# Third stage of a four-stage layer: whole score blocks below the diagonal in four 32-row tiles, numerators split in every fourth step

## The chip, the cores and the metric

The kernel runs on one core of a Trainium2 chip. The metric is the time of one execution on the device in microseconds (us). Five engines run their own instruction queues in order: PE multiplies matrices (PEld is its loading of the stationary operand), DVE, ACT and POOL work on vectors, SP issues transfers.

## The reference

The input is a tensor of 2 batches x 1024 tokens x 128 features, held in fp32. Four blocks follow one another, each as x = x + LN(block(LN(x))), with LN a layer norm without gain. The change touches the third block alone, a causal attention with 16 heads of 8 features and a linear position bias:

```
q = (x @ Wq + bq).reshape(B, S, 16, 8)          # k and v alike
scores = einsum('bthd,bshd->bhts', q, k) / sqrt(8)
scores = scores - slope[h] * |s - t|            # slope 2**(-8/16*(h+1))
scores = where(s > t, -inf, scores)
out = einsum('bhts,bshd->bthd', softmax(scores), v).reshape(B, S, 128)
return out @ Wo + bo
```

The first block is a non-causal attention with 8 heads, the second a mixture of experts, the fourth two layers of a local attention with a gated feed-forward part.

## The kernel before

The stages `phase1` to `phase4` run one after another. `phase3` (from line 705) works on eight groups u = 0 to 7: two batches times four groups of four heads. Lines named here are those of the kernel before.

**Operands.** `make(u, "q")` and `make(u, "k")` (lines 821 to 844) project the tokens of one batch onto the four heads of a group. They use three matmuls for each half of 512 tokens (high and low parts of both operands, `mm3`). The weights hold every head's 8 columns three times, so that the stacked operand `stk` (128 rows x 1024 tokens, fp16) has 32 rows of rounded values, 32 rows that are either the rounding's rest or a second copy, 32 more of this kind, and in rows 96 to 127 constants loaded from memory (`c_rows3`). These are 8 rows a head: the position bias in pieces, and one row that carries minus the row maximum. One product over 128 rows thus gives four heads' scores added up. To keep the heads apart, k is copied four times into `kz`, each copy multiplied by a column of `pick` that is zero outside one head's rows (lines 838 to 842, two of the four on POOL and two on DVE, except in the first group, where DVE does all).

**Maxima.** `max_pass` (lines 853 to 869) computes scores with the queries on the partitions, 128 queries by up to 512 keys. Blocks on the diagonal get the causal mask by a second matmul (line 864). DVE reduces each bank to a negative maximum (line 869). `units` lists the pieces of a group, 38 in all. `max_rows(u, c)` (lines 871 to 879) transposes the maxima of one half of the queries on PE into partitions 96 to 127 of a bank, and one ACT copy writes them from there into rows 96 to 127 of q.

**Scores.** `scores(n)` (lines 883 to 904) computes one step: 12 steps a group, step (c, j) for query half c and key block j of 128, with the keys on the partitions. Steps (0, 0) to (0, 3) and (1, 4) to (1, 7) touch the diagonal; (1, 0) to (1, 3) are whole blocks of 512 queries. There are four matmuls, one for each head, against `kz`; ACT's exponential (line 898) reads the bank into `pt`, of which there are four buffers. In every second step ACT copies `pt` to fp16 (line 902) and POOL subtracts (line 903): `hl` holds a high and a low part.

**Values.** `values(n)` (lines 906 to 931) multiplies by V, four heads side by side in 32-column tiles: with `hl`, two fp16 passes against V in fp16; without, `pt` and V in fp32. A `pt` without `hl` is free again only after this. `outputs` (line 933) divides by the sums and, after its matmuls (line 942), writes the result.

**Order.** The main loop (lines 977 to 1003) runs over steps m from -12 to the end. The maxima run 12 steps ahead of the scores and the values four steps behind them:

```
            if 0 <= m < steps:
                put(scores, m)
            ...
            for unit in rows:
                put(max_rows, *unit)
            ...
            if 0 <= m - 4 < steps:
                put(values, m - 4)
            while done < len(todo) and done < (u + 1) * len(units) / 12:
                put(max_pass, *todo[done])
```

Here `u` is m + 12, and after the maxima come `make` for the next group (at steps 3 and 5 of twelve), `finish` and `outputs`. `put` chains PE's instructions, so PE follows the written order. The order on ACT, DVE, POOL and SP is set by a planner from planned times, within the dependences. `k.tick` (line 1003) lets the fourth stage's preparation in from m = 54 on: loads on SP (line 1056 is its weights'), and on POOL and ACT the splitting of weights (lines 1058 to 1063).

**Banks.** `bank()` (line 786) takes PSUM banks in turn from two pools of three. In the last 14 steps it takes them from one pool of three only.

Of the kernel before, what the change touches and what calls it, by code (L numbers as in the profile page):

```python
# [704 lines left out]
def phase3(k, X):  # L705
# [5 lines left out]
    with ExitStack() as es:  # L711
# [14 lines left out]
        bias = cp.tile([96, 2, G], F32, name="bias")  # L726
        nc.sync.dma_start(bias, A["t_bqk3"])
        scale = HD**-0.5
        nc.vector.tensor_scalar(bias[:, 0, :], bias[:, 0, :], scale, None, ALU.mult)
        bvo = cp.tile([128, 2, D], F32, name="bvo")  # L730
        for i, n in enumerate(("bv", "bo")):
            nc.sync.dma_start(bvo[:, i, :], A["L1_attn_" + n].partition_broadcast(128))
        wqk = {}
        for i, n in enumerate("qk"):
            w = work().rearrange("p t d -> p (t d)")[:, : G * 96].rearrange("p (g m) -> p g m", g=G)
# [85 lines left out]
        def make(u, n):  # L821
            b, g = u // G, u % G
            xTh, xTl = S["x", b]
            wh, wl = wqk[n]
            i = 0 if n == "q" else 1
            stk = qp.tile([128, N], F16, name=n + "st", bufs=3 if n == "q" else 1)
            S["dma"] = nc.sync.dma_start(stk[96:128, :], A["c_rows3"][i, g])
            bc = bias[:, i, g : g + 1]
            lo = slice(32, 64) if n == "q" else slice(64, 96)
            for c in range(2):  # L830
                s = slice(512 * c, 512 * c + 512)
                ps = bank()
                k.mm3(ps[:96, :], wh[:, g, :], wl[:, g, :], xTh[:, s], xTl[:, s])
                nc.scalar.activation(stk[:96, s], ps[:96, :], AF.Identity, bias=bc)
                nc.vector.scalar_tensor_tensor(stk[lo, s], ps[lo, :], bc[lo, :], stk[lo, s], ALU.add, ALU.subtract)
            if n == "k":
                kz = qp.tile([128, 4, N], F16, name="kz")
                for a in range(4):
                    if u and a < 2:
                        S["kz"] = nc.gpsimd.tensor_scalar(kz[:, a, :], stk, pick[:, a : a + 1], None, ALU.mult)  # L840
                    else:
                        nc.vector.tensor_scalar(kz[:, a, :], stk, pick[:, a : a + 1], None, ALU.mult)
                stk = kz
            S[n, u] = stk


        units = []
        for t in range(NT):
            for e in range(t // 4 + 1):
                m = {1: 4, 2: 2}.get(t + 1 - 4 * e, 1)  # L850
                units += [(t, e, a, m) for a in range(0, 4, m)]

        def max_pass(u, i):
            t, e, a0, m = units[i]
            n = 128 * min(4, t + 1 - 4 * e)
            ps = bank().rearrange("p (a n) -> p a n", a=m)
            q0, kz = S["q", u], S["k", u]
            diag = e == t // 4
            for a in range(m):
                nc.tensor.matmul(  # L860
                    ps[:, a, :n], q0[:, 128 * t : 128 * t + 128], kz[:, a0 + a, 512 * e : 512 * e + n], start=True, stop=not diag
                )
                if diag:
                    nc.tensor.matmul(ps[:, a, n - 128 : n], identb, causal[:, 0, :], start=False, stop=True)  # L864
            if e == 0:
                out = mx[:, u % G, t, :].rearrange("p (a r) -> p a r", r=8)[:, a0 : a0 + m, 6]
            else:
                out = mx2[:, u % 2, t - 4, a0 : a0 + m]
            S["max"] = nc.vector.tensor_reduce(out, ps[:, :, :n], AX.X, ALU.max, negate=True)  # L869
# [12 lines left out]

        def scores(n):
            u = n // 12
            c, j = order[n % 12]
            q1, kz = S["q", u], S["k", u]
            s = max(512 * c, 128 * j)
            w = 512 * c + 512 - s
            diag = j >= 4 * c
            pt = pp.tile([128, 4, 512], F32, name="pt")  # L890
            m = {128: 4, 256: 2}.get(w, 1)
            for a0 in range(0, 4, m):
                st = bank().rearrange("p (a n) -> p a n", a=m)
                for a in range(m):
                    nc.tensor.matmul(st[:, a, :w], kz[:, a0 + a, 128 * j : 128 * j + 128], q1[:, s : s + w], start=True, stop=not diag)  # L895
                    if diag:
                        nc.tensor.matmul(st[:, a, :128], identb, causal[:, 1, :], start=False, stop=True)  # L897
                S["exp"] = nc.scalar.activation(pt[:, a0 : a0 + m, :w], st[:, :, :w], AF.Exp)  # L898
            hl = None
            if n % 2 == 0:  # L900
                hl = pp.tile([128, 2, 4, 512], F16, name="hl", bufs=2)
                nc.scalar.copy(hl[:, 0, :, :w], pt[:, :, :w])  # L902
                nc.gpsimd.tensor_tensor(hl[:, 1, :, :w], pt[:, :, :w], hl[:, 0, :, :w], ALU.subtract)  # L903
            S["p", n] = pt, hl, s, w
# [65 lines left out]
        ahead = 12  # L970
        for n in "qk":
            make(0, n)
        done = 0
# [585 lines left out]
def consts():  # L1559
# [26 lines left out]
    c["c_pick3"] = (np.arange(128)[:, None] // 8 % 4 == np.arange(4)).astype(np.float32)  # L1586
# [46 lines left out]
def layouts(inputs):  # L1633
# [11 lines left out]
    w = np.stack([a["L1_attn_" + n].reshape(128, 4, 1, 32) for n in ("Wq", "Wk")], 1)  # L1645
    c["t_wqk3"] = np.repeat(w, 3, 3).reshape(128, 2, 4, 96)
    w = np.stack([a["L1_attn_" + n].reshape(4, 32) for n in ("bq", "bk")])
    c["t_bqk3"] = np.concatenate([w, w, w], 2).transpose(2, 0, 1)
# [29 lines left out]
```

## Time and profile before

| | |
|---|---|
| time, median of 3 runs | 1354.97 us (1350.28 to 1356.17) |
| profiled execution | 1356.68 us |
| its span (first to last instruction) | 1354.9 us |
| mean granted TensorE clock | 0.945 |
| busy, share of the span | PE 86%, PEld 53%, DVE 72%, ACT 71%, POOL 62% |
| chain that ended last, by engine | PE 42%, DVE 29%, ACT 14%, issue 6%, POOL 4%, DMA 3% |
| line 898, exponentials | x304, 480 to 668 ns |
| line 869, maxima | x304, 540 to 700 ns |
| line 902, copies of the numerators | x48, 1045 to 1980 ns |
| line 903, their rests on POOL | x48, 2125 to 4095 ns |
| line 827, constant rows | x16, 64 KB each, 1.8 us from issue to landing |

All durations come from the one profiled execution. A matmul's duration holds its way through the array; matmuls that follow each other closely start sooner than that, so distances between starts are given where they matter. Line 49, 50 and 51 are the helper `mm3`, which all stages use. The windows give, for a stretch of the span, how long each engine was busy.

### The profile page before, as it was taken

The page shows a single profiled execution, that of the slowest core. Times are in us where ns is not written, and L with a number is a line of the kernel's source. Part 1 is how long each engine was busy: PE and PEld are TensorE (multiplying, and loading weights), DVE is VectorE, ACT ScalarE, POOL GpSimd, SP SyncE. Part 2 cuts the span into 40 slices and gives each one's busy share as a digit, 9 for nine tenths or more (in the row PEclk, how much of TensorE's full clock was granted, in tenths as well). Part 3 has the DMA queues.
Part 4 walks back from the last instruction along what each step waited for, and adds up shares of the span by engine and source line. Part 5 has one row for each costly group of instructions (what it writes and reads, how often), then busy time and mean ns, then how long its engine had stood idle before and what let it go on. Part 6 is the DMA issues. An engine that isn't in the chain of part 4 may idle for free.

```text
span 1354.9 us, 28455 instructions
## 1 busy us (share of the span) xinstructions
PE 1162.4 (86%) x11558; PEld 716.5 (53%) x11558; DVE 982.3 (72%) x1970; ACT 958.2 (71%) x1481; POOL 842.6 (62%) x525
## 2 busy tenths in 40 slices
PE   4799999999897889887799998798668898998886
PEld 1366666666565646443355544343336565666564
DVE  6777666776674385989888789571578887888855
ACT  2777777787686364541898987789367788887755
POOL 1666667777665463733676768785577886666611
PEclk8899999999898999998999999898679899999999
DMA  2000000000000031300000013000157666555520
GB/s 77 1 2 2 2 2 1 2 17 18 1 1 2 18 131 32 112 13 4 3 5 3 5 38 73 1 21 1 24 94 163 122 119 106 103 99 100 106 59 16
DMA packets 123394, 57.59 MB, mean 43 GB/s; under 512 B 105568, under 2 KB 114800, under 8 KB 123264
## 3 DMA queue, kind: packets, MB, share of 16 engines
q1 hardware_dynamic: 121360, 54.50, 18.7%
q8 instruction: 90, 1.47, 0.4%
q10 hardware_dynamic: 1472, 1.09, 0.3%
q0 software_dynamic: 432, 0.20, 0.2%
q14 instruction: 40, 0.33, 0.1%
HBM read 21.69 MB, written 1.11 MB: 17 GB/s over the span
## 4 chain that ended last, share of the span: by engine, by line
PE 42%; DVE 29%; ACT 14%; issue 6%; POOL 4%; DMA 3%; SPq 0%; POOLq 0%; DVEq 0%; ACTq 0%
DVE mx L869 5%; PE big L360 5%; PE pu L49 4%; PE pu L51 3%; PE pu L50 3%; DVE nm L332 3%; PE pu L920 3%; ACT pt L898 2%; PE big L49 2%; PE big L51 2%; PE big L50 2%; PE bank L895 1%; PE bank L860 1%; PE big L656 1%; DVE ln_st L81 1%
## 5 line engine op out<-in xcount | busy, mean ns | idle before, releaser
L367 POOL TENSOR_TENSOR hl<-p,hl 128x1024 f16<-128x1024 f32 x128 | 274.0, 2143 | 142.8 <-ACT hl L366 116.2
L903 POOL TENSOR_TENSOR hl<-pt,hl 128x2048 f16<-128x2048 f32 (+1 forms) x48 | 164.4, 3432 | 78.1 <-ACT hl L902 68.4
L332 DVE TENSOR_REDUCE nm<-big 128x2 f32<-128x1024 f32 x128 | 155.2, 1220 | 32.3 <-PE big L329 31.6
L364 ACT ACTIVATE p<-big 128x1024 f32<-128x1024 f32 x128 | 130.9, 1023 | 52.4 <-PE big L360 51.6
L49 PEld LDWEIGHTS <-hl 128*128 128x128 f16 x1024 | 100.5, 98 | 75.7 <-DVE acc L392 43.6
L366 ACT CAST hl<-p 128x1024 f16<-128x1024 f32 x128 | 133.8, 1045 | 4.1
L869 DVE TENSOR_REDUCE mx<-bank 128x1 f16<-128x512 f32 (+3 forms) x157 | 102.1, 653 | 32.1 <-PE bank L860 16.4
L869 DVE TENSOR_REDUCE mx<-bankz 128x1 f16<-128x512 f32 (+3 forms) x147 | 96.6, 660 | 18.7 <-PE bankz L864 12.8
L898 ACT ACTIVATE pt<-bank 128x512 f32<-128x512 f32 (+1 forms) x172 | 97.0, 582 | 18.5 <-PE bank L897 11.1
L49 PE MATMUL pu<-V1h,hl 128*128 128x129 f16 x512 | 92.6, 224 | 12.4 <-DVE acc L392 11.7
L49 PE MATMUL pu<-V0h,hl 128*128 128x129 f16 x512 | 93.1, 224 | 10.8 <-DVE acc L392 9.5
L50 PEld LDWEIGHTS <-hl 128*128 128x128 f16 x1024 | 101.3, 99 | 0.0
L1221 POOL TENSOR_TENSOR rot<-rot,rn 128x512 f32<-128x512 f32 x64 | 66.3, 1056 | 55.8 <-DVE rn L1211 50.4
L51 PEld LDWEIGHTS <-hl 128*128 128x128 f16 x1024 | 100.5, 98 | 0.0
L1196 POOL TENSOR_TENSOR rot<-rot,t 128x512 f32<-128x512 f32 x64 | 84.1, 1326 | 20.2 <-DVE t L1190 20.1
L51 PE MATMUL pu<-V0h,hl 128*128 128x129 f16 x512 | 92.5, 223 | 0.0
L50 PE MATMUL pu<-V0l,hl 128*128 128x129 f16 x512 | 92.5, 222 | 0.0
L51 PE MATMUL pu<-V1h,hl 128*128 128x129 f16 x512 | 92.0, 222 | 0.0
L50 PE MATMUL pu<-V1l,hl 128*128 128x129 f16 x512 | 92.0, 221 | 0.0
L898 ACT ACTIVATE pt<-bankz 128x512 f32<-128x512 f32 (+1 forms) x132 | 76.8, 583 | 20.8 <-PE bankz L897 9.9
L88 POOL TENSOR_TENSOR ln_rstd<-ln_rs,nhalf 128x4 f32<-128x4 f32 (+2 forms) x29 | 32.8, 1135 | 81.4 <-DVE ln_rs L84 67.3
L895 PE MATMUL bank<-qst,kz 128*128 128x512 f16 (+3 forms) x218 | 68.1, 345 | 13.5 <-DVE mx L869 7.5
(412 smaller groups left out, 3730.9 us busy)
## 6 DMA issues: line engine op xcount, KB each, us to landing
sb<-sd SPq DMA_DIRECT2D x16, 512.0 KB, 4.4
Vs<-V SPq DMA_DIRECT2D x60, 130.0 KB, 2.4
work<-in_t_w SPq DMA_DIRECT2D x2, 512.0 KB, 3.5
out<-F SPq DMA_DIRECT2D x3, 256.0 KB, 2.3
X<-in_L_attn_x SPq DMA_DIRECT2D x2, 256.0 KB, 3.3
w<-in_t_wqk SPq DMA_DIRECT2D x1, 512.0 KB, 5.1
wv<-in_t_wv ACTq DMA_DIRECT2D x1, 512.0 KB
X<-in_L_attn_x ACTq DMA_DIRECT2D x1, 512.0 KB, 5.0
```

The lines of the kernel that those rows point to most:

```text
L49: mm(out, lh, rh, start=start, stop=False, **kw)
L50: mm(out, lh, rl, start=False, stop=False, **kw)
L51: mm(out, ll, rh, start=False, stop=stop, **kw)
L332: S["red"] = nc.vector.tensor_reduce(S["n", u][:, i // 2, c, :], ps, AX.X, ALU.max, negate=True)
L364: S["exp"] = nc.scalar.activation(p, st, AF.Exp, scale=QSCALE**-2)
L366: nc.scalar.copy(hl[:, 0], p)
L367: S["lo"] = nc.gpsimd.tensor_tensor(hl[:, 1], p, hl[:, 0], ALU.subtract)
L869: S["max"] = nc.vector.tensor_reduce(out, ps[:, :, :n], AX.X, ALU.max, negate=True)
L895: nc.tensor.matmul(st[:, a, :w], kz[:, a0 + a, 128 * j : 128 * j + 128], q1[:, s : s + w], start=True, stop=not diag)
L898: S["exp"] = nc.scalar.activation(pt[:, a0 : a0 + m, :w], st[:, :, :w], AF.Exp)
L903: nc.gpsimd.tensor_tensor(hl[:, 1, :, :w], pt[:, :, :w], hl[:, 0, :, :w], ALU.subtract)
L1196: eng("ra" if j else "rb", i).tensor_tensor(rot[:, j], rot[:, j], t2[:, j], ALU.add)
```

## The change

The rows of the operands are put in another order. Each head now has 32 adjacent rows: three times its 8 features (rounded values and rests) and its 8 constant rows. The weights get a fourth, empty set of columns, so that a projection fills all 128 rows. ACT writes the projection, multiplied by a column `low` that is one on the rows that need the rest, into a new tile `hi`; one DVE pass over 128 rows then makes `stk` out of both. The constant rows come after that, by four transfers of 8 rows each. `k`'s operand gets three buffers and is kept beside `kz`.

A new helper `four` takes the four heads of a whole block: four matmuls over 32 rows each, in four tile positions, into four banks, and then the four readers. Whole blocks in `max_pass` and `scores` use it with the unmultiplied operand; blocks on the diagonal keep `kz`. In `units` a whole block is now one unit with a load of 4, and the loop counts loads. `max_rows` copies the maxima to a tile `mr`, from which four transfers on SP take them to q's rows. The numerators are split where n is a multiple of 4.

```diff
+        low = cp.tile([128, 2], F32, name="low")
+        nc.sync.dma_start(low, A["c_low3"])
...
+        lbias = cp.tile([128, 2, G], F32, name="lbias")
+        nc.vector.tensor_tensor(lbias, bias, low.unsqueeze(2).to_broadcast([128, 2, G]), ALU.mult)
...
-            h = cp.tile([128, G, 96], F32R, name=n + "wh")
-            l = cp.tile([128, G, 96], F32R, name=n + "wl")
+            h = cp.tile([128, G, 128], F32R, name=n + "wh")
+            l = cp.tile([128, G, 128], F32R, name=n + "wl")
...
-            stk = qp.tile([128, N], F16, name=n + "st", bufs=3 if n == "q" else 1)
-            S["dma"] = nc.sync.dma_start(stk[96:128, :], A["c_rows3"][i, g])
+            stk = qp.tile([128, N], F16, name=n + "st")
             bc = bias[:, i, g : g + 1]
-            lo = slice(32, 64) if n == "q" else slice(64, 96)
             for c in range(2):
                 s = slice(512 * c, 512 * c + 512)
                 ps = bank()
-                k.mm3(ps[:96, :], wh[:, g, :], wl[:, g, :], xTh[:, s], xTl[:, s])
-                nc.scalar.activation(stk[:96, s], ps[:96, :], AF.Identity, bias=bc)
-                nc.vector.scalar_tensor_tensor(stk[lo, s], ps[lo, :], bc[lo, :], stk[lo, s], ALU.add, ALU.subtract)
+                k.mm3(ps, wh[:, g, :], wl[:, g, :], xTh[:, s], xTl[:, s])
+
+                hi = qp.tile([128, 512], F16, name="hi", bufs=2)
+                nc.scalar.activation(hi, ps, AF.Identity, scale=low[:, i : i + 1], bias=lbias[:, i, g : g + 1])
+                nc.vector.scalar_tensor_tensor(stk[:, s], ps, bc, hi, ALU.add, ALU.subtract)
+            for a in range(4):
+                S["dma"] = nc.sync.dma_start(stk[32 * a + 24 : 32 * a + 32, :], A["c_rows3"][i, g, 8 * a : 8 * a + 8])
...
+        def four(l, r, w, use):
+
+            tiles = [bank() for _ in range(4)]
+            for a, ps in enumerate(tiles):
+                d = slice(32 * a, 32 * a + 32)
+                nc.tensor.matmul(ps[:, :w], l[d, :], r[d, :], start=True, stop=True, tile_position=(32 * a, 0))
+            for a, ps in enumerate(tiles):
+                use(a, ps[:, :w])
...
-                m = {1: 4, 2: 2}.get(t + 1 - 4 * e, 1)
+                m = {1: 4, 2: 2}.get(t + 1 - 4 * e, 1) if e == t // 4 else 4
                 units += [(t, e, a, m) for a in range(0, 4, m)]
+        load = [4 if e < t // 4 else 1 for t, e, *_ in units]
...
+            if e < t // 4:
+                four(q0[:, ts], kst[:, 512 * e : 512 * e + n], n, lambda a, ps: reduce(a, ps.unsqueeze(1)))
+                return
...
-            nc.scalar.copy(S["q", u][96:128, 512 * c : 512 * c + 512], ps[96:128, :])
+            mr = qp.tile([128, 512], F16, name="mr", bufs=2)
+            nc.scalar.copy(mr[96:128, :], ps[96:128, :])
+            q = S["q", u][:, 512 * c : 512 * c + 512]
+            for a in range(4):
+                nc.sync.dma_start(q[32 * a + 24 : 32 * a + 32, :], mr[96 + 8 * a : 104 + 8 * a, :])
...
+            if not diag:
+                four(kst[:, ks], q1[:, s : s + w], w, lambda a, ps: exp(a, ps.unsqueeze(1)))
...
-            if n % 2 == 0:
+            if n % 4 == 0:
                 hl = pp.tile([128, 2, 4, 512], F16, name="hl", bufs=2)
...
-            while done < len(todo) and done < (u + 1) * len(units) / 12:
+            while done < len(todo) and spent < (u + 1) * sum(load) / 12:
                 put(max_pass, *todo[done])
+                spent += load[todo[done][1]]
                 done += 1
```

More of the change, by code (lines that the diff above doesn't have):

```diff
@@ L725, in phase3 @@
         nc.sync.dma_start(both, A["c_both3"])
-        bias = cp.tile([96, 2, G], F32, name="bias")
+        low = cp.tile([128, 2], F32, name="low")
+        nc.sync.dma_start(low, A["c_low3"])
+        bias = cp.tile([128, 2, G], F32, name="bias")
         nc.sync.dma_start(bias, A["t_bqk3"])
@@ L734, in phase3 @@
         for i, n in enumerate("qk"):
-            w = work().rearrange("p t d -> p (t d)")[:, : G * 96].rearrange("p (g m) -> p g m", g=G)
+            w = work().rearrange("p t d -> p (t d)")[:, : G * 128].rearrange("p (g m) -> p g m", g=G)
             nc.sync.dma_start(w, A["t_wqk3"][:, i])
-            h = cp.tile([128, G, 96], F32R, name=n + "wh")
-            l = cp.tile([128, G, 96], F32R, name=n + "wl")
+            h = cp.tile([128, G, 128], F32R, name=n + "wh")
+            l = cp.tile([128, G, 128], F32R, name=n + "wl")
             if n == "q":
@@ L842, in make @@
                         nc.vector.tensor_scalar(kz[:, a, :], stk, pick[:, a : a + 1], None, ALU.mult)
-                stk = kz
+                S["z", u] = kz
             S[n, u] = stk
+        def four(l, r, w, use):
[5 more added lines that the diff above has]
+                use(a, ps[:, :w])
         units = []
@@ L855, in max_pass, with reduce @@
             n = 128 * min(4, t + 1 - 4 * e)
+            q0, kst, kz = S["q", u], S["k", u], S["z", u]
+            if e == 0:
+                out = mx[:, u % G, t, :].rearrange("p (a r) -> p a r", r=8)[:, :, 6]
+            else:
+                out = mx2[:, u % 2, t - 4, :]
+            ts = slice(128 * t, 128 * t + 128)
+            def reduce(a, ps):
+                S["max"] = nc.vector.tensor_reduce(out[:, a : a + ps.shape[1]], ps, AX.X, ALU.max, negate=True)
+            if e < t // 4:
+                four(q0[:, ts], kst[:, 512 * e : 512 * e + n], n, lambda a, ps: reduce(a, ps.unsqueeze(1)))
+                return
             ps = bank().rearrange("p (a n) -> p a n", a=m)
-            q0, kz = S["q", u], S["k", u]
-            diag = e == t // 4
             for a in range(m):
[L860 to L869, printed above, removed]
+                nc.tensor.matmul(ps[:, a, :n], q0[:, ts], kz[:, a0 + a, 512 * e : 512 * e + n], start=True, stop=False)
+                nc.tensor.matmul(ps[:, a, n - 128 : n], identb, causal[:, 0, :], start=False, stop=True)
+            reduce(a0, ps[:, :, :n])
         def max_rows(u, c):
@@ L885, in scores @@
             c, j = order[n % 12]
-            q1, kz = S["q", u], S["k", u]
+            q1, kst, kz = S["q", u], S["k", u], S["z", u]
             s = max(512 * c, 128 * j)
@@ L890, in scores, with exp @@
             pt = pp.tile([128, 4, 512], F32, name="pt")
+            ks = slice(128 * j, 128 * j + 128)
+            def exp(a, ps):
+                S["exp"] = nc.scalar.activation(pt[:, a : a + ps.shape[1], :w], ps, AF.Exp)
+            if not diag:
+                four(kst[:, ks], q1[:, s : s + w], w, lambda a, ps: exp(a, ps.unsqueeze(1)))
             m = {128: 4, 256: 2}.get(w, 1)
-            for a0 in range(0, 4, m):
+            for a0 in range(0, 4 if diag else 0, m):
                 st = bank().rearrange("p (a n) -> p a n", a=m)
                 for a in range(m):
[L895 to L898, printed above, removed]
+                    nc.tensor.matmul(st[:, a, :w], kz[:, a0 + a, ks], q1[:, s : s + w], start=True, stop=False)
+                    nc.tensor.matmul(st[:, a, :128], identb, causal[:, 1, :], start=False, stop=True)
+                exp(a0, st[:, :, :w])
             hl = None
-            if n % 2 == 0:
+            if n % 4 == 0:
                 hl = pp.tile([128, 2, 4, 512], F16, name="hl", bufs=2)
@@ L972, in phase3 @@
             make(0, n)
-        done = 0
+        done = spent = 0
         later = chain(tokens(1), values_of(1))
@@ L1585, in consts @@
     c["c_mx3"] = mx.reshape(128, 4, NT, 32)
-    c["c_pick3"] = (np.arange(128)[:, None] // 8 % 4 == np.arange(4)).astype(np.float32)
+    c["c_pick3"] = (np.arange(128)[:, None] // 32 == np.arange(4)).astype(np.float32)
+    part = np.arange(128) % 32 // 8
+    c["c_low3"] = np.stack([part == 1, part == 2], 1).astype(np.float32)
     both = np.zeros((128, 4, 9), np.float32)
@@ L1644, in layouts @@
     c["t_wv"] = a["L0_attn_Wv"].reshape(8, 128, 128).transpose(2, 0, 1)
[L1645 to L1648, printed above, removed]
+    three = lambda v: np.concatenate([v, v, v, np.zeros_like(v)], -1)
+    w = np.stack([a["L1_attn_" + n].reshape(128, 4, 4, 8) for n in ("Wq", "Wk")], 1)
+    c["t_wqk3"] = three(w).reshape(128, 2, 4, 128)
+    w = np.stack([a["L1_attn_" + n].reshape(4, 4, 8) for n in ("bq", "bk")])
+    c["t_bqk3"] = three(w).reshape(2, 4, 128).transpose(2, 0, 1)
     pad = lambda v: np.concatenate([v, np.zeros((*v.shape[:-1], 384 - v.shape[-1]), v.dtype)], -1)
```

## The prediction

> **What bounds the kernel now.** The page gives no single answer (PE 86%, DVE 72%, ACT 71%, POOL 62% of the span), so I read the third stage by windows. Its matmuls begin at 601 us and end at 964 us. Scores start at 641, and seven of the eight head groups run with the maxima of the next group beside them until 917; the eighth runs alone.
>
> ```profile
> 655.00:674.20 19.20, 17.12 (x123) 7.63 (x122) 15.71 (x26) 17.53 (x29) 12.93 (x5) 0.99 0.01 3
> 674.20:820.00 145.80, 138.96 (x1197) 73.47 (x1197) 117.20 (x221) 131.25 (x209) 105.36 (x35) 1.00 0.04 12
> 820.00:858.00 38.00, 32.20 (x270) 17.27 (x270) 32.97 (x75) 29.55 (x51) 22.93 (x12) 1.00 0.27 65
> 858.00:880.00 22.00, 14.05 (x102) 6.42 (x102) 10.88 (x19) 15.68 (x26) 21.92 (x11) 0.86 0.00 1
> 880.00:917.00 37.00, 34.64 (x296) 17.20 (x295) 26.07 (x46) 32.91 (x55) 31.88 (x12) 0.95 0.06 19
> 917.00:956.00 39.00, 33.68 (x229) 14.20 (x226) 5.95 (x14) 33.66 (x55) 21.35 (x7) 0.78 0.00 1
> ```
>
> The columns after the length are PE, PEld, DVE, ACT, POOL, granted clock, DMA share, GB/s. In 674–820 PE is busy 95% and ACT 90%: both are nearly full. The output matmuls of line 942 cut each group of twelve steps in two: they close steps 4 and 8. Steps 5 to 8 (part A) and steps 9 to 4 of the next group (part B) read thus (three A, then two B):
>
> ```profile
> 696.14:710.25 14.11, 13.01 (x95) 6.01 (x93) 11.12 (x21) 13.97 (x23) 11.40 (x4) 1.00 0.02 7
> 735.12:748.96 13.84, 12.63 (x93) 5.70 (x90) 11.01 (x20) 13.67 (x22) 10.96 (x4) 1.00 0.02 3
> 770.75:784.40 13.65, 12.43 (x91) 5.54 (x89) 10.85 (x20) 13.51 (x22) 10.79 (x4) 1.00 0.01 3
> ...
> 674.19:696.14 21.95, 21.52 (x207) 11.70 (x205) 16.86 (x32) 19.41 (x33) 15.22 (x5) 1.00 0.02 5
> 748.96:770.75 21.79, 21.35 (x206) 11.53 (x204) 16.70 (x31) 19.23 (x31) 15.20 (x5) 1.00 0.02 6
> ```
>
> Part A is ACT's: 13.7 of 13.9 us. Part B, where all but one block lies on the diagonal, is PE's: 21.4 of 21.9 us. So a microsecond taken from ACT counts in A alone, one taken from PE in B alone. The two rest on different edits.
>
> **The copies of the numerators.** Step n splits pt into hl now when n is a multiple of 4, not of 2. Each group loses the splits of n = 2, 6 and 10 (256, 512 and 256 queries wide). The groups by form, 600–960:
>
> ```profile
> L903 POOL TENSOR_TENSOR hl<-pt,hl 128x2048 f16<-128x2048 f32 x32 | 130.4, 4080 | 68.2 <-ACT hl L902 58.6 <-PE bankz L895 9.4
> L902 ACT CAST hl<-pt 128x2048 f16<-128x2048 f32 x32 | 60.8, 1901 | 1.3 <-PE pu L920 0.4
> L902 ACT CAST hl<-pt 128x1024 f16<-128x1024 f32 x16 | 16.7, 1046 | 0.5
> ```
>
> ACT loses 1.90 + 2 × 1.05 = 4.0 us a group, POOL 4.08 + 2 × 2.14 = 8.4. One 1.90 lies in A, the rest in B, where ACT has 2.4 us to spare.
>
> **What PE pays for it.** These steps now multiply the fp32 numerators. Either way the timeline has eight instructions for the four heads: 512 wide they take 1.05 us in fp32 (786.24) and 0.61 split (789.03): +0.43. For 256 wide the split takes 0.40; fp32 lies between 0.41 (128 wide) and 0.83 (384 wide), so about 0.62: +0.22. A step's values run four steps later, so n = 2 falls into A (+0.22), n = 6 and 10 into B (+0.65).
>
> **Four heads side by side.** Whole blocks below the diagonal are eight quadruples of 512-wide matmuls a group, four in scores, four in the maxima. By the new load count the maxima's come in steps 4, 5, 6 and 9, the scores' in steps 4 to 7: five in A, three in B. Four in sequence start 0.215 us apart, 0.86 together. No 32-row tile is in this trace; the nearest rows are the first stage's pairs of 64-row tiles:
>
> ```profile
> 202.89 0.39 PE L360 MATMUL big<-qh,kh 64*128 64x512 f16 x2
> ...
> 203.11 0.38 PE L360 MATMUL big<-ql,kh 64*128 64x512 f16 x2
> ...
> 203.76 0.38 PE L329 MATMUL big<-kh,qh 64*128 64x512 f16 x2
> ...
> 204.07 0.10 PEld L49 LDWEIGHTS <-hl 128*128 128x128 f16 x1 [0.42 <-DVE acc L392]
> ```
>
> Two matmuls take the time of one (0.22 from pair to pair), and the next full-height work follows 0.31 after the last pair began, 0.1 late. So a quadruple saves at most 3 × 0.215 = 0.65 us, and at least 0.44 with 0.1 lost on the way in and out. I take 0.55, the middle, because some 0.1 is also lost on the way into the 32-column tiles of line 920 (the last block before starts at 786.09, lasts 0.06 to the next, and they start at 786.24). If tiles of 32 rows did not overlap at all, it saves nothing.
>
> On this the Trainium skill speaks twice. "TensorEngine Tiling (Array Packing)", section Key Properties, says that changing the tiling mode drains TensorE: that is the rule against this change, and the 0.1 us above is what this trace shows of it. "TensorE: Matmul & The Clock Gate", Part 3, gives 3.07 times for four 32-row tiles at 512 columns; by that a quadruple would take 0.28 and save 0.58. No run here shows that figure.
>
> **Sum per group.** A: ACT 13.7 − 1.9 = 11.8; PE 12.7 − 5 × 0.55 + 0.2 = 10.1; DVE stays at 11.0, since every quadruple still needs four reductions (0.60 apart). ACT would allow 12.0; with DVE so near, and the numerators' four buffers now freed by values instead of by the copy in three more steps, I take 12.5: −1.4, between −1.9 and 0. B: PE −3 × 0.55 + 0.65 = −1.0, between −1.3 and +0.65. Together −2.4 a group; the seven groups make −16.8.
>
> **The other terms.** In 858–880 the chain runs through POOL (hl 3.68, kz 5.69, acc 2.77, tab, hl 4.03) and PE is idle for 8 us; half of the splits gone takes a 4.07 subtraction out of it: −3, between −6 and 0. The last group (917–956) is split between ACT (33.7 of 39) and PE: ACT −4.0, PE +0.9 at a clock of 0.78, and with three banks left the fourth tile must wait for the first exponential: −2, between −4 and +1. At the start, the constant rows of q and k now land after the vector pass: four issues of 0.31 and 1.8 to landing are 3.0 us, where kz followed within 0.3 us. DVE has layer norm work to put there: +2, between 0 and +3. Weights padded from 96 to 128 columns: +0.5 at most.
>
> **Edits taken at nothing.** The projection's activation and vector pass keep their 512 columns (0.68 and 0.74). In steady state k's rows cost the same 3.0 us: they land at 780.6 instead of 777.6; POOL's two kz then end at 786.3, and the maxima need them seven steps later, some 20 us. But DVE's two kz (778.36) are queued in order: reductions stand behind them, and PE waits for banks behind those. If the planner leaves them where they are, DVE stands for 2.3 us in A. The row maxima no longer go from ACT straight into q: a copy, four transfers, again 3.0 us. For the second half the copy ends at 763.69 and the first score that reads it starts at 767.93: 4.2 us of cover, 1.2 to spare. If that goes, PE stands, eight times.
>
> **Total.** −16.8 − 2 − 3 + 2.5 = −19.3. The span of 1354.9 becomes 1335.6, and the profiled execution, 1.8 above its span (1356.68), 1337.4. The median of the three runs is 1.7 below that execution: 1336 us.
>
> **Rivals.** (1) *SP's queue, slower.* Today q's maxima don't pass through SP; now eight transfers a group do, in order, beside the loads for the fourth stage:
>
> ```profile
> SPq L1056 <- POOL wql L1063: 51.3, 1, 51.3
> ...
> SPq L1056 <- POOL wvl L1063: 13.6, 1, 13.6
> ```
>
> The first wait is 834–885, and the copies at 841.28 and 853.52 fall into it; the score that needs the first starts at 848.39. If that load is placed ahead of the rows, PE stands until 885 + 3: nearly 40 us, less the 20 gained: about 1373. Behind the second wait alone (copy at 890.88) it is some 6 us: 1342. It decides as soon as the planner thinks POOL quicker than it is by the length of such a wait. Against: the load hangs on wql, which stands behind the seventh kz on POOL, and both copies come before that in the order written. Chance 0.20.
> (2) *Gain eaten.* DVE's kz waits (2.3 × 7 = 16 us at most, half of it in slack), or the quadruples gain nothing: then B is +0.65 a group and A gains 0.9 at most. 1341 to 1355. Chance 0.22; the transfer cover above is thin, and the pairs of 64 rows speak against the second half.
> (3) *More.* Both A and B follow their engine fully and the POOL stall goes: −(1.9 + 1.3) × 7 − 6 − 4 = −32: 1323. DVE at 11.0 of 12 in A speaks against. Chance 0.12.
>
> **How the numbers follow.** Forecast (1326 to 1344) 0.46. Half a per cent, 6.8 us, is about what a measurement of this kernel can tell. Faster by more, below 1348: 0.46 + 0.12 + 0.09 of rival 2 = 0.67. Within: 0.13. Slower: 0.20. The range runs from 1318 to 1367: it holds the bounds of the terms and the weaker half of rival 1, and leaves out under 0.2.
>
> **What would show it.** Right: splits x24 on ACT and POOL; ACT about 32 us and POOL about 67 us less busy; quadruples of 32x512 starting within some 0.05 us; A about 12.5 and B about a microsecond shorter; SP's issues up by 112, none waiting on POOL ahead of a row of q. Wrong: A unchanged with DVE waiting for a transfer before kz; quadruples 0.2 us apart; PE standing for q after 834; the 858–880 stall unchanged.

## The result and the profile after

The changed kernel takes 1373.04 us (median of four runs, 1371.63 to 1376.82), against 1354.72 for the kernel before: a ratio of 1.0145 (95% interval 1.0113 to 1.0177). The forecast was 1336 us, its range ended at 1367, and "slower" had a chance of 0.20. The direction was wrong. All line numbers from here on are those of the changed kernel, unless "before" is said.

The busy times of the page came out near the forecast: ACT is busy for 25.9 us less than before (958.2; about 32 were forecast), POOL for 64.3 less (842.6; about 67), PE for the same.

```profile
PE 1161.6 (85%) x11558; PEld 711.1 (52%) x11558; DVE 978.9 (71%) x1971; ACT 932.3 (68%) x1457; POOL 778.3 (57%) x501
```

The groups of the third stage by form show why. The full-width splits on POOL are 24 of 4.08 us, not 32, and the 16 of half width are gone. POOL now waits for the constant rows ahead of its copies of k (line 846), 42.8 us in all:

```profile
L933 POOL TENSOR_TENSOR hl<-pt,hl 128x2048 f16<-128x2048 f32 x24 | 97.8, 4076 | 127.1 <-issue 73.2 <-ACT hl L932 53.7
L846 POOL TENSOR_SCALAR kz<-kst,pick 128x1024 f16<-128x1024 f16 x14 | 40.8, 2920 | 42.8 <-DMA kst<-in_c_rows 42.8
```

The timeline of PE in step 5 (start, duration) shows the four tiles of the scores side by side, since four banks are free (736.3), and those of the maxima in pieces, since they are not (a pair at 737.4, one tile at 738.8, one at 739.3):

```profile
736.32 0.38 PE L857 MATMUL bank<-qst,kst 32*128 32x512 f16 x1
736.33 0.39 PE L857 MATMUL bankz<-qst,kst 32*128 32x512 f16 x1
736.33 0.38 PE L857 MATMUL bank<-qst,kst 32*128 32x512 f16 x1
736.33 0.39 PE L857 MATMUL bankz<-qst,kst 32*128 32x512 f16 x1
...
737.41 0.38 PE L857 MATMUL bank<-kst,qst 32*128 32x512 f16 x1
737.42 0.39 PE L857 MATMUL bankz<-kst,qst 32*128 32x512 f16 x1
738.76 0.55 PE L857 MATMUL bank<-kst,qst 32*128 32x512 f16 x1 [0.96 <-ACT pt L918]
739.25 0.58 PE L857 MATMUL bankz<-kst,qst 32*128 32x512 f16 x1
```

The last two took 0.55 and 0.58, not 0.38: the clock had just fallen. The windows of the same parts as in the prediction (three A, one B, then two of the late stretches; columns as there, the granted clock third from the end):

```profile
695.31:708.85 13.54, 12.08 (x95) 5.63 (x93) 10.47 (x19) 12.59 (x23) 7.35 (x3) 1.00 0.06 15
735.36:750.63 15.27, 13.62 (x91) 5.95 (x89) 10.83 (x18) 12.05 (x21) 7.62 (x3) 0.78 0.05 12
774.24:787.59 13.35, 11.42 (x91) 5.08 (x89) 10.61 (x18) 12.09 (x21) 5.74 (x2) 1.00 0.06 15
671.70:695.31 23.61, 22.42 (x207) 11.28 (x205) 17.59 (x32) 17.17 (x29) 10.33 (x3) 1.00 0.01 2
...
858.00:880.00 22.00, 15.64 (x97) 6.70 (x95) 12.98 (x21) 17.44 (x32) 9.74 (x3) 0.74 0.29 74
...
917.00:956.00 39.00, 24.83 (x192) 10.65 (x191) 9.79 (x20) 24.28 (x43) 13.84 (x4) 0.84 0.01 1
```

Part A is 13.4 to 13.5 us where the clock stays at 1.00 (13.7 to 14.1 before) and 15.3 where it is 0.78. Part B is 23.6 instead of 21.95, although ACT's work in it fell from 19.4 to 17.2. In 917 to 956, which now lies almost wholly in the last group, both PE and ACT are busy for less than 25 of 39 us: as the waits below show, ACT stands for POOL and for PE.

The same is seen from the output matmuls that close steps 4 and 8 (line 972, before 942). From the first to the one that opens the last group they span 245.7 us (before 235.5), and the last group takes 67.8 us from there to its end (before 56.8): 917.4 to 985.3 instead of 909.6 to 966.4. The stage ends 18.9 us later; the fourth stage gives 3.6 of it back, and the span grows by 15.3 us.

The waits of ACT in the third stage (in all, times, longest) name two releasers that grew, PE's values (line 950) and POOL's subtraction (line 933). After:

```profile
ACT pt L918 <- PE pu L950: 25.0, 22, 4.1
...
ACT pt L918 <- POOL hl L933: 18.1, 10, 4.2
```

Before:

```profile
ACT pt L898 <- PE pu L920: 9.0, 11, 2.8
ACT pt L898 <- POOL hl L903: 7.3, 2, 5.5
```

Three of the waits for POOL are 4.2 us long and lie in the last group. On ACT's timeline, each split there (line 932) is followed at once by a stand until POOL is through (two of the three):

```profile
932.13 1.90 ACT L932 CAST hl<-pt 128x2048 f16<-128x2048 f32 x1
938.19 1.65 ACT L918 ACTIVATE pt<-bank 128x384 f32<-128x384 f32 x4 [4.16 <-POOL hl L933]
...
947.24 1.90 ACT L932 CAST hl<-pt 128x2048 f16<-128x2048 f32 x1
953.36 2.06 ACT L918 ACTIVATE pt<-bank 128x512 f32<-128x512 f32 x4 [4.22 <-POOL hl L933]
```

The written order explains this. The values of step n are issued after the scores of step n+4, so when a step asks for one of the four buffers of `pt`, those of the four steps before it are all still held, except where a step was split: its buffer is free once POOL has subtracted. With a split in every fourth step three buffers are held, and step 4i+1 has only the one of the step just before it: its exponential must wait for that step's copy on ACT (1.90) and subtraction on POOL (4.08). With a split in every second step two buffers circulated.

### The profile page after: what moved, and what is told of

It reads as the page before. It is cut to its first block, busy times and chain, and to the rows that moved or that the text cites. A ratio compares the mean times of both kernels' runs of the same rounds, so it can differ in the third digit from the quotient of the medians.

```text
span 1370.2 us, 28539 instructions
## 1 busy us (share of the span) xinstructions
PE 1161.6 (85%) x11558; PEld 711.1 (52%) x11558; DVE 978.9 (71%) x1971; ACT 932.3 (68%) x1457; POOL 778.3 (57%) x501
## 5 line engine op out<-in xcount | busy, mean ns | idle before, releaser
L933 POOL TENSOR_TENSOR hl<-pt,hl 128x2048 f16<-128x2048 f32 x24 | 97.8, 4076 | 127.1 <-issue 73.2
L846 POOL TENSOR_SCALAR kz<-kst,pick 128x1024 f16<-128x1024 f16 x14 | 40.8, 2920 | 42.8 <-DMA kst<-in_c_rows 42.8
```

## The experiments

Each time is a median with its ratio to runs of the kernel before (1350.4 to 1353.1 us) on the same chip. Three theories stood at the start: (A) the buffers of the numerators; (B) the new order of the rows, its transfers and the tiles; (C) the fp32 numerators that PE has to multiply.

**Tiles and rows without the fewer splits.**

```diff
-            if n % 4 == 0:
+            if n % 2 == 0:
```

> Tiles and new row layout kept, numerators split in every second step again. Theory A (buffers): with one split in four steps, three of the four numerator buffers wait for values and the fourth for POOL's subtraction, so the exponentials stand; then this run loses the stands of 4.2 us on POOL in the last group and is 1330 to 1350 us, faster than before. Theory B (layout): the rows by transfer and the tiles themselves cost the time; then it stays near 1370. Theory C (fp32 on PE): the fp32 values cost PE some 0.65 us in each part of steps 9 to 4; then it is about 1360.

Measured 1371.47 us, 1.0144 (1.0128 to 1.0159). The tiles and rows alone cost about as much as the whole change; theory A by itself falls.

**The fewer splits without tiles and rows** (the kernel before, edited).

```diff
-            if n % 2 == 0:
+            if n % 4 == 0:
```

> The kernel before with nothing changed but the split: every fourth step. Theory A: the exponentials stand as in the changed kernel, without what the tiles give back; 1370 to 1385 us, with waits of ACT on POOL's subtraction in the last group of about 4 us each. Theory B: this edit is free or a gain, 1340 to 1355. Theory C: PE pays 0.87 us a group, 7 us in all, about 1362, and ACT does not wait for POOL.

Measured 1356.97, 1.0042 (1.0026 to 1.0058). No gain either, although ACT loses the same 4.0 us a group, and the time lies in the range of none of the three theories. Theory A's waits are there: ACT stands for POOL's subtraction for 20.6 us in all, 4.2 at most. The last group begins 5.1 us earlier than before (904.5 against 909.6), but takes 9.6 us longer (66.4 against 56.8). So both halves of the change cost time, each alone, and the costs do not add up.

**A fifth buffer for the numerators in the changed kernel**, paid for with one of two buffers of `hl`.

```diff
-            pt = pp.tile([128, 4, 512], F32, name="pt")
+            pt = pp.tile([128, 4, 512], F32, name="pt", bufs=5)
...
-                hl = pp.tile([128, 2, 4, 512], F16, name="hl", bufs=2)
+                hl = pp.tile([128, 2, 4, 512], F16, name="hl", bufs=1)
```

> The changed kernel with five numerator buffers instead of four; to make room the split's tile has one buffer instead of two. Theory A: a step's exponentials find a free buffer without waiting for values or POOL; the three stands of 4.2 us in the last group go, and steps 9 to 4 lose their stands on values; 1335 to 1352. Theory B and theory C: no change, 1368 to 1376.

Measured 1355.06, 1.0014 (0.9992 to 1.0036): 18 us less than the changed kernel, 3 above theory A's range. The ten runs spread from 1348.4 to 1362.5, and the profiled one is among the shorter (1350.74). Its last group takes 52.2 us instead of 67.8. The waits of ACT in the third stage no longer hold POOL's subtraction or the values among the nine largest; what is left is TensorE's scores:

```profile
ACT pt L918 <- PE bankz L927: 27.2, 16, 11.3
ACT pt L918 <- PE bank L927: 21.1, 20, 2.9
```

**Values issued ahead of the scores**, so that a buffer comes free one step earlier.

```diff
+            if 0 <= m - 4 < steps:
+                put(values, m - 4)
             if 0 <= m < steps:
                 put(scores, m)
...
-            if 0 <= m - 4 < steps:
-                put(values, m - 4)
```

> The changed kernel with the values of step m - 4 put on PE ahead of the scores of step m instead of behind them, all else the same. Theory A: the buffer that the exponentials need is free by the time their scores are, also in the last group; 1335 to 1355. Theory B and theory C: the same instructions, no change beyond 5 us: 1365 to 1378.

Measured 1359.4, 1.0059 (1.0042 to 1.0076): 14 us of the same loss by another road, slightly above the forecast. The last group takes 48.9 us. That the buffers are held too long is thus shown in two ways.

**The rows without the tiles.** The helper `four` uses the full height and `kz`, with the split in every second step; the units of four remain.

```diff
-            tiles = [bank() for _ in range(4)]
-            for a, ps in enumerate(tiles):
-                d = slice(32 * a, 32 * a + 32)
-                nc.tensor.matmul(ps[:, :w], l[d, :], r[d, :], start=True, stop=True, tile_position=(32 * a, 0))
-            for a, ps in enumerate(tiles):
+            for a in range(4):
+                ps = bank()
+                nc.tensor.matmul(ps[:, :w], l(a), r(a), start=True, stop=True)
                 use(a, ps[:, :w])
```

> The changed kernel's order of rows, its loads and copies of rows by transfer, its start and its units of four banks, but every whole block multiplied at full height with kz, and numerators split in every second step. It differs from e1_split2 (1371.5 us) in the 32-row tiles alone. Theory L (the new order of the rows costs it: start, transfers, projections): 1366 to 1374. Theory T (the quadruples cost it: four banks asked for within 0.01 us, and a clock that falls when TensorE has less to do): 1352 to 1360, with part A at a clock of 1.00 and some 14 us long, and the first exponential still 3 to 6 us late.

Measured 1363.25, 1.0078 (1.0057 to 1.0100). Between the theories: of e1's 20 us, 11 come without any 32-row tile, 8 with the tiles. As theory T had it, the first three parts A run at a clock of 1.00 and take 14.1 to 14.6 us.

**The last group's subtraction on DVE** instead of POOL.

```diff
-                nc.gpsimd.tensor_tensor(hl[:, 1, :, :w], pt[:, :, :w], hl[:, 0, :, :w], ALU.subtract)
+                (nc.vector if n >= 84 else nc.gpsimd).tensor_tensor(hl[:, 1, :, :w], pt[:, :, :w], hl[:, 0, :, :w], ALU.subtract)
```

> The changed kernel, with the subtraction of the numerators' split on DVE instead of POOL in the last group (three of them, steps 84, 88 and 92), where DVE has little to do. Theory A (the next exponential waits for POOL's subtraction, since the other three buffers hold fp32 numerators): the three waits of 4.2 us of ACT there shrink to about 1 to 2.2, so 1363 to 1367. Rival (the three banks of the last group bind it): 1371 to 1376, the waits of ACT turning into waits for TensorE.

Measured 1376.68, 1.0178 (1.0161 to 1.0196): the forecast of the time failed. The part that the edit touches did what theory A said: DVE's subtraction takes 2.2 to 2.3 us, ACT's three waits fell from 4.2 to 2.5, 2.5 and 2.8, and the last group from 67.8 to 61.5 us. But it began at 926.9 instead of 917.4. The first part A, which the edit does not touch, took 16.0 us at a clock of 0.81 where the changed kernel had 13.5 at 1.00. In the two traces every engine issues the same instructions in the same order until 934 us, so these 9.5 us come with the clock, which fell at other places: they lie in parts A. Between two kernels with tiles in the maxima a difference of this size need not come from the edit.

**The split in every fourth step and the fifth buffer, without tiles and rows.** The kernel of e2 with e3's two edits.

```diff
-            pt = pp.tile([128, 4, 512], F32, name="pt")
+            pt = pp.tile([128, 4, 512], F32, name="pt", bufs=5)
...
-            if n % 2 == 0:
-                hl = pp.tile([128, 2, 4, 512], F16, name="hl", bufs=2)
+            if n % 4 == 0:
+                hl = pp.tile([128, 2, 4, 512], F16, name="hl", bufs=1)
```

> The kernel before with the split in every fourth step (e2_only4, 1357.0 us) and five buffers for the numerators, paid for with one buffer less for hl. Theory A (a buffer that stays fp32 is held four steps, and that took the gain of the fewer splits): 1335 to 1348, without ACT waiting for POOL's subtraction. Rival (the buffers bind only together with the tiles): 1354 to 1360.

Measured 1331.29, 0.9838 (0.9809 to 0.9868), the fastest of all kernels here, below theory A's range: the fewer splits are worth 21 us once the numerators have a fifth buffer, and the buffer alone makes 25.7 us against e2, with no tile in either kernel. Its last group takes 48.9 us (before 56.8, e2 66.4). Part B and part A by the windows:

```profile
670.00:692.20 22.20, 21.84 (x206) 11.71 (x205) 16.90 (x31) 16.89 (x29) 8.15 (x2) 1.00 0.02 7
...
692.20:705.50 13.30, 12.65 (x96) 6.00 (x93) 11.11 (x21) 12.82 (x23) 9.82 (x3) 1.00 0.01 2
```

**The rows without the units of four.** The maxima's whole blocks one head at a time again.

```diff
-                m = {1: 4, 2: 2}.get(t + 1 - 4 * e, 1) if e == t // 4 else 4
+                m = {1: 4, 2: 2}.get(t + 1 - 4 * e, 1)
...
-        load = [4 if e < t // 4 else 1 for t, e, *_ in units]
+        load = [1 for _ in units]
```

> e5_rows_only (1363.3 us, 11 above the kernel before) with the maxima's whole blocks given out one head at a time again, as in the kernel before, instead of four heads at once. Left of the change: the order of the rows, their transfers and the later start. Theory U (units of four are started early, up to three reductions ahead of their share, so that part B, which TensorE and DVE fill, gets 12 whole-block matmuls instead of 8): part B back from 23.3 to about 22.0 us, 1352 to 1357. Theory R (the rows' transfers and POOL's later copies of k cost it): part B stays at 23, 1360 to 1365.

Measured 1366.93, 1.0115 (1.0095 to 1.0134). Theory U falls: without the units of four it is no faster than e5. With four buffers and a split in every second step the rows alone cost 16 us. POOL, busy for 17.8 of 22.8 us in part B, waits for the rows' transfer ahead of its copies of k (before, in the same window: 0.9 us, for DVE):

```profile
POOL kz L846 <- DMA kst<-in_c_rows: 19.1, 6, 4.2
```

and PE waits in turn for the numerators that POOL splits behind them (before: 6.3 us, in one wait):

```profile
PE pu L950 <- POOL hl L933: 8.5, 7, 1.8
```

PE's wait grew by far less than the time did, so that the queue on POOL makes up the 16 us is not shown; the first part A also ran at a clock of 0.91 and took 16.6 us.

**Every 32-row matmul twice**, in e1's kernel.

```diff
+                for _ in range(2):
-                nc.tensor.matmul(ps[:, :w], l[d, :], r[d, :], start=True, stop=True, tile_position=(32 * a, 0))
+                    nc.tensor.matmul(ps[:, :w], l[d, :], r[d, :], start=True, stop=True, tile_position=(32 * a, 0))
```

> e1_split2 (1371.5 us; granted clock 0.93 in 700 to 800 us, where e5_rows_only with full-height matmuls has 1.00) with every matmul of a 32-row tile issued twice, so that TensorE works some 0.25 us longer in each of the 64 quadruples, 16 us in all. Theory C (the clock is lowered because TensorE is left with too little to do between the waits for banks): the clock in 700 to 800 rises to 0.98 or more, part A shrinks by about a microsecond in spite of the added work, and the time falls to 1360 to 1370. Rival (the clock does not hang on that, the work just adds where TensorE binds, in part B): 0.93 as before and 1374 to 1382.

Measured 1373.08, 1.0166 (1.0131 to 1.0201). Half of theory C held. Part A at e1, with every matmul once:

```profile
699.21:714.25 15.04, 13.36 (x96) 5.97 (x93) 10.47 (x19) 14.56 (x24) 8.60 (x3) 0.89 0.05 13
739.69:755.38 15.69, 13.75 (x91) 5.99 (x89) 10.12 (x18) 14.14 (x23) 8.39 (x3) 0.78 0.04 12
```

and with every matmul twice:

```profile
700.00:714.80 14.80, 13.91 (x115) 5.90 (x113) 10.88 (x19) 14.10 (x23) 8.27 (x3) 1.00 0.05 13
741.00:755.30 14.30, 12.93 (x111) 5.41 (x109) 10.51 (x18) 13.60 (x22) 8.06 (x3) 1.00 0.05 13
```

More work made the clock stay at 1.00 in these parts and part A shorter, by 0.2 and 1.3 us from output to output. The first three parts B grew by 0.7 to 1.1 us, and the clock still fell later on (first at 833, again after 873), so the time did not follow.

**The rows and the fifth buffer** (e8 with the split in every fourth step and e3's two edits).

> e8 with the split in every fourth step and five buffers for the numerators: e7_only4_pt5 (1331.3 us) plus the order of the rows alone. Theory R (the rows by transfer cost time at any setting of the buffers): 1338 to 1346. Theory U (only the units of four and the tiles cost): 1331 to 1336.

Measured 1334.12, 0.9870 (0.9848 to 0.9891). The rows, 16 us in e8, cost 2.8 here, as theory U had it. That POOL, relieved by fewer splits, and the spare buffer hide their later arrival is the likely reason; no run separates the two.

**Tiles in the scores alone, with the fifth buffer** (e3 with e8's edit of the units, and the maxima's whole blocks at full height).

```diff
-                four(q0[:, ts], kst[:, 512 * e : 512 * e + n], n, lambda a, ps: reduce(a, ps.unsqueeze(1)))
+                ps = bank()
+                nc.tensor.matmul(ps[:, :n], q0[:, ts], kz[:, a0, 512 * e : 512 * e + n], start=True, stop=True)
+                reduce(a0, ps[:, :n].unsqueeze(1))
```

> e3_pt5 (the changed kernel with five buffers, 1355.1 us) with the maxima's whole blocks at full height and one head at a time again, so that only the scores use the 32-row tiles. It differs from e10 in the scores' tiles alone. If the units of four in the maxima are what costs (they ask DVE for four reductions at once, and the clock falls behind them): 1330 to 1340, at or below e10. If the tiles themselves cost: 1345 to 1355, near e3_pt5 and above e10.

Measured 1336.70, 0.9894 (0.9875 to 0.9912). The scores' tiles add 2.6 us to e10, if anything, and save nothing: part B is 22.1 us in both. In the second part A of e11 PE is busy for 11.2 us, a microsecond less than in e10, and that part takes 12.7 us against 12.5; ACT has 12.2 and 12.1 us of work in it.

**Units of four at full height, with the fifth buffer.** Only the maxima's matmuls differ from e3.

```diff
-                four(q0[:, ts], kst[:, 512 * e : 512 * e + n], n, lambda a, ps: reduce(a, ps.unsqueeze(1)))
+                tiles = [bank() for _ in range(4)]
+                for a, ps in enumerate(tiles):
+                    nc.tensor.matmul(ps[:, :n], q0[:, ts], kz[:, a, 512 * e : 512 * e + n], start=True, stop=True)
+                for a, ps in enumerate(tiles):
+                    reduce(a, ps[:, :n].unsqueeze(1))
```

> e3_pt5 (1355.1 us) with the maxima's whole blocks still given out four heads at once, into four banks before the four reductions, but multiplied at full height with kz; the scores keep their 32-row tiles. It stands between e3_pt5 and e11 (1336.7 us, the same but one head at a time). If the units of four cost the 18 us between them: 1350 to 1357. If the 32-row tiles of the maxima cost them (TensorE too little at work while DVE frees bank after bank, and the granted clock falls: 0.95 in 700 to 800 us of e3_pt5, 1.00 in e11): 1335 to 1341, with the clock there at 1.00.

Measured 1338.39, 0.9887 (0.9861 to 0.9912). So the 32-row tiles of the maxima cost 16.7 us, and the units of four 1.7, which is not told from nothing. The windows of the first three parts A, and then of three microseconds around step 6 in which scores and maxima both wait for banks, here at full height:

```profile
693.80:707.40 13.60, 12.31 (x97) 5.86 (x94) 10.53 (x19) 12.56 (x23) 7.23 (x3) 1.00 0.05 14
732.70:745.70 13.00, 11.47 (x92) 5.29 (x90) 10.00 (x18) 11.96 (x21) 7.01 (x3) 1.00 0.05 13
768.50:781.50 13.00, 11.47 (x92) 5.28 (x90) 10.51 (x17) 11.96 (x21) 5.64 (x2) 1.00 0.06 15
...
701.20:704.20 3.00, 2.51 (x12) 0.74 (x11) 3.00 (x6) 2.22 (x6) 0.00 (x0) 1.00 0.09 25
```

and in e3, in tiles:

```profile
696.30:712.30 16.00, 14.58 (x95) 6.24 (x93) 10.83 (x20) 14.53 (x24) 9.51 (x3) 0.82 0.05 12
738.10:751.20 13.10, 11.13 (x93) 5.09 (x90) 10.04 (x18) 12.16 (x22) 6.89 (x2) 1.00 0.05 13
773.80:788.10 14.30, 12.55 (x92) 5.76 (x90) 10.11 (x18) 12.19 (x22) 6.89 (x2) 0.88 0.05 14
...
703.80:706.80 3.00, 2.35 (x12) 0.80 (x11) 3.00 (x6) 2.51 (x6) 0.00 (x0) 0.93 0.09 25
706.80:708.80 2.00, 2.00 (x13) 0.54 (x13) 1.92 (x4) 1.91 (x5) 1.92 (x1) 0.50 0.00 0
```

In the second part A, where e3's clock stays at 1.00, the tiles cost nothing (13.0 us from output to output in both); in the other two, at 0.82 and 0.88, e3 is 2.5 and 1.2 us longer. DVE is busy for the whole of the three microseconds in both, so the tiles cannot run ahead of it. PE is busy for 2.35 instead of 2.51 us, and then, in e3, the clock halves for what follows. On e3's timeline the last tiles of the scores, which wait for banks that DVE still reads for the maxima, come 0.60 apart, and the full-height scores after them take 0.63 (0.38 at full clock) and start 0.53 apart (0.28 in e12, 704.79 to 705.07):

```profile
706.19 0.41 PE L857 MATMUL bank<-qst,kst 32*128 32x512 f16 x1 [0.23 <-DVE mx L880]
706.79 0.58 PE L857 MATMUL bankz<-qst,kst 32*128 32x512 f16 x1 [0.19 <-DVE mx L880]
...
708.35 0.63 PE L926 MATMUL bankz<-qst,kz 128*128 128x512 f16 x1
708.78 0.31 PE L927 MATMUL bankz<-causal,identb 128*128 128x128 bf16 x1
708.88 0.63 PE L926 MATMUL bank<-qst,kz 128*128 128x512 f16 x1
```

Over the whole stage e3's last output matmul begins 11.5 us after e12's, and of that 11.1 lie ahead of the first output (2.5) and in four parts A in which its clock fell (2.5, 1.2, 1.8 and 3.0). In e3's windows of these five stretches (for the first the 13.5 us ahead of the output) the granted clock is 0.75, 0.82, 0.88, 0.90 and 0.65, in e12's it is 1.00 throughout. In a fifth part A (856.2 to 872.0) e3's clock was 0.78 and cost only 0.3. The two traces as a whole lie 9.8 us apart (spans of 1348.0 and 1338.2), not 16.7: e3's profiled run was 4.3 us faster than its median, e12's 1.6 slower, so the rest of the 16.7 lies in runs without a trace here.

Over all kernels the fall goes with the single tiles of the maxima. In 700 to 800 us the clock fell in all five traces that have them (the change, e1, e3, e4 and e6: 0.93 to 0.97), and in one of the nine others (e8: 0.98; the rest 1.00).

## Why the prediction was wrong, point by point

The pieces put together, in us: from 1352 the fewer splits with a fifth buffer lead to 1331 (e7). From there the rows add 2.8 (e10), the scores' tiles 2.6 (e11), the units of four 1.7 (e12) and the maxima's tiles 16.7 (e3). Going back to four buffers adds 18 and gives the 1373 of the change. Steps of 2 to 3 us are within what two such medians can differ: by the ratios to the kernel before on the same chip the four steps are 4, 3, −1 and 17 us. Only the 21, the 17 and the 18 are clear of that, and by the traces the 17 is the clock's; the 18 may hold some of it too.

**The buffers: the term that was mis-sized.** The prediction named them ("freed by values instead of by the copy in three more steps") and gave them, with DVE, half a microsecond of part A. It did not ask which buffer is free when a step asks, and so missed that step 4i+1 can only have the one in POOL's hands. By the medians it cost 18 us with the tiles (the change against e3) and 25.7 without (e2 against e7). In the traces of the change and e3 the last group alone differs by 15.6 us (67.8 against 52.2); there no maxima fill the wait. The last group was forecast at −2 and came out at +11.

**The copies.** Their size was right (ACT 25.9 of 32 us and POOL 64.3 of 67 less), and so was that they are worth something: e7 gained 21 us, the stretch around 858–880 and the last group included. But with four buffers none of it arrived. A part of ACT's shortfall is an edit taken at nothing: the projection's activation takes 0.78 us instead of 0.68, 32 times.

**The quadruples.** Where four banks are free they run side by side as forecast, but the 0.55 us was not saved: PE's 10.1 us in A came out at 11.4 to 12.1 even at full clock. In A, ACT (and DVE, for the maxima) empties the banks; e11 gains nothing for a microsecond less of PE. In B the three quadruples were worth 1.65 by the sum. With the scores' one, part B is 22.1 us in e11 as in e10 without; with the maxima's two it is 22.7 in e3, against 22.8 in e12 without. The Trainium skill has this rule: "TensorEngine Tiling (Array Packing)", section PSUM Bottleneck, says that tiling makes TensorE faster but not the emptying of PSUM. The traces agree (tiles 0.5 to 0.6 us apart behind ACT and DVE); the prediction weighed only the drain, about 0.1 us, which was right.

**The clock: the step that was missing.** The sum took the granted clock of 1.00 from the trace before and kept it. No rival had it fall. With the maxima in tiles it fell in one of the first three parts A of the changed kernel, in all three of e1, and in two of e3's, where it cost 2.5 and 1.2 us against e12. "TensorE: Matmul & The Clock Gate", Part 1, says that the clock is halved after an idle window of some 3.4 us. In e3 it fell with no gap between matmuls over 0.4 us in the ten microseconds ahead, so that rule does not cover the case. The section "A second HAM failure mode: psum-queue depth-cycling" of that page, where short waits between groups of matmuls make the clock swing, is nearer to what was measured here.

**Part B.** Forecast −1.0, measured +1.7: +0.7 comes with the units of four (22.1 in e11, 22.8 in e12), and +0.9 with the buffers (22.75 in e3, 23.6 in the change). The prediction's count of three quadruples in B was right, and the kernel before has as many whole blocks there (12 matmuls in both traces). So the units of four change their order, not their number; why that costs 0.7 is open.

**The rows.** DVE's copies of k hardly waited; POOL's did, 42.8 us. What that cost the changed kernel was not isolated; in e10, with fewer splits and five buffers, the rows cost 2.8 us in all. PE waits for the rows of q for 3.0 us in e10, and the changed kernel's trace shows no such wait: the prediction's cover held. Rival 2 was right that the quadruples gain nothing and that gains would be eaten, but its range ended at 1355: it had neither the buffers nor the clock. **SP's queue**, the slower rival, ended near the measured time and was wrong too: the load behind POOL's weights waited 12.8 us, once, not 51. **The start**: the first exponential came 3.2 us later (2.5 forecast), yet the first output 2.3 us earlier. **858–880**: POOL's chain went (21.9 to 9.7 us), but the part A that holds this stretch, from 860.9 to 882.5, took 21.6 us at a clock of 0.68, against 16.4 at 0.90 before.

## What to carry to other kernels

When a change makes a buffer live longer, write down for each step which buffers are still held when it asks for one, and who frees the one that it gets; a single extra buffer decided here between +5 and −21 us. The tiles were worth nothing here, where other engines empty TensorE's banks, and with them TensorE lost its clock for the full-height work that followed: look for the granted clock in the stretch itself. Try the parts of a change apart: the good half of this one was worth 1.6%, with the one buffer that it lacked, and was buried under two others.

## What was not expected of the hardware

The granted clock halved in a stretch of e3 in which PE was busy for 78% (2.35 of 3.00 us, no wait over 0.23 us), and not in the same stretch at 84% (e12). But the busy time that the profile shows does not decide it. In e11, where the maxima have their full height, the clock stayed at 1.00 after a stretch with PE busy for 62% and a wait of 1.28 us:

```profile
700.40:703.80 3.40, 2.12 (x19) 0.90 (x11) 3.34 (x6) 3.33 (x7) 2.60 (x1) 1.00 0.01 3
```

In e9 it halved at 958.8 after one at 93%, most of it eight matmuls of 32 rows:

```profile
955.40:958.80 3.40, 3.15 (x19) 0.82 (x20) 0.00 (x0) 3.37 (x8) 2.98 (x2) 1.00 0.03 7
```

That 32-row matmuls count for less fits both; no run isolates it, and where the limit lies is open. A quadruple also costs two very different amounts: its four matmuls start within 0.01 us with four free banks, and are spread over 1.8 us (737.41 to 739.25) without.
